# A two-layer expert network on one core: fetching one of each token's two answers during the last expert

## The chip, the cores and the metric

The kernel runs on one core of a Trainium2 chip. A core has five engines with queues of their own: TensorE (PE; its weight loads are listed as PEld), VectorE (DVE), ScalarE (ACT), GpSimd (POOL) and SyncE (SP). Each engine works its queue off in order. Transfers are started from the queues of SP, ACT and POOL and are carried out by 16 DMA engines that all queues share. The metric is the device time of one execution in microseconds, as the median over runs.

## The reference, cut to what matters

Eight sequences of 100 tokens (800 tokens of width 512) pass through two layers. Each layer has a cross-attention and then an expert network in which a router picks two of eight experts for each token. The first expert network is the one at issue:

```python
xf = layernorm(x) * gamma + beta
probs = softmax(xf @ Wg.T + bg)
tp, ti = top_k(probs, 2)
tp = tp / (sum(tp) + 1e-8)
w = sum(one_hot(ti, 8) * tp[..., None], axis=1)
h = gelu(einsum('td,efd->tef', xf, W1) + b1)
y = einsum('tef,edf->ted', h, W2) + b2
x = x + einsum('ted,te->td', y, w)
```

A token needs the answers of its two experts only, each times its own weight. After this comes the second layer's cross-attention, which begins with a layer norm of the new `x`.

## The kernel before

Everything is in float32. The 800 tokens lie in seven tiles of 128 rows (the last one has 32), and `x` stays in SBUF all the time.

**Routing (class Route).** As the tokens' tiles are ready, `group` finds for each token its best and its second expert, works out a row number in a table for each, and sends the normalised token to both rows with indirect DMAs from the POOL queue (L267). `where[0]` and `where[1]` hold these row numbers and `m[0]`, `m[1]` the weights: index 0 is the better expert of a token, index 1 the second best. The table `sent` and the table of results, `answers`, have 800 rows for each expert.

**Order of the experts.** `order` (L274) counts the tokens of each expert and numbers the experts by size: the one with most tokens gets slot 0 and is worked off first, that with the fewest gets slot 7. The weights are prefetched in this order through a pool of eight tiles, from SP's queue.

**Working the experts off (`work_off`, L379).** For each slot, `arrived` fetches the tokens' rows from `sent` and turns them into columns. `hidden0` makes the hidden activations on PE and ACT in four groups of matmuls. After the first group it calls `between`, which turns the previous expert's result back into rows and writes it to `answers` from the POOL queue (`returned`, L377). `products` makes the second matmul. When the loop is through, the last expert's result is written.

**The conditional rest (`rest`, L394).** If an expert has more tokens than its slot holds, a conditional block works the remainder off. With these inputs it is jumped over. On the way past it each engine makes up for the semaphore counts of the block that it skipped (events at L397), and POOL first waits for all transfers of its own queue.

**Between the expert layer and the attention.** `project_early` (L449) makes keys and values of five units of the second batch's context for the attention that follows: for each unit 2 x 4 matmuls into PSUM (L425), two ACT copies to `mT` (L429), six transposes (L437), three ACT copies to `mv` (L439 to L442) and three stores from ACT's queue. In the same stretch both answers of each token are fetched from `answers` (`fetch`, L333, an indirect DMA from POOL's queue), two fetches for each of the seven tiles, and DVE adds each of them, times its weight, to `x` (L723). Then each tile gets its moments (L127, L129), a square root on ACT (L137), its normalised copy `xn` (L146), four transposes on PE (L157) and four ACT evictions into `xT1` (L166). POOL adds the output bias to `x` (L729). A scheduler of the framework interleaves the instructions of this stretch on each engine; what it put first on an engine's queue blocks what it put behind.

The tiles for the fetched rows have two buffers, each with room for both answers of a token tile. The `xn` tiles have two buffers as well, and so have the small tiles of factors.

The second layer's attention begins with the query projection (L414), which needs `xT1` whole.

Of the kernel before, what the change touches and what calls it, by code (L numbers as in the profile page):

```python
# [13 lines left out]
P = 128  # L14
# [52 lines left out]
def two_layers(ctx: ExitStack, tc: tile.TileContext, a: dict, out: bass.AP):  # L67
# [137 lines left out]
    class Route:  # L205


        def __init__(self, layer, psum, tag):
            self.layer, self.psum, self.tag = layer, psum, tag
            self.logits = routes.tile([P, NTILE, NE], F32, tag="logits", name=f"logits{layer}")  # L210
            nc.vector.memset(self.logits, 0.0)
            self.m = [routes.tile([P, NTILE], F32, tag=f"m{k}", name=f"m{k}_{layer}") for k in range(2)]
            self.where = [
                routes.tile([P, NTILE], mybir.dt.int32, tag=f"where{k}", name=f"where{k}_{layer}") for k in range(2)
            ]
            self.sel = routes.tile([P, NTILE, NE], F32, tag="sel", name=f"sel{layer}")
# [6 lines left out]

        def largest(self, v, m, name):

            g = v.shape[1]
            nc.vector.tensor_reduce(m, v, AX.X, ALU.max)
            at = self.temp([P, NTILE, NE], f"at{name}")[:, :g, :]
            nc.vector.tensor_tensor(at, v, over_experts(m), ALU.is_equal)
            nc.vector.tensor_tensor(at, at, rank.unsqueeze(1).to_broadcast([P, g, NE]), ALU.mult)  # L230
            first = self.temp([P, NTILE], "first")[:, :g]
            nc.vector.tensor_reduce(first, at, AX.X, ALU.max)
            nc.vector.tensor_tensor(at, at, over_experts(first), ALU.is_equal)
            return at

        def group(self, i0, i1, xn):

            g, v = i1 - i0, self.logits[:, i0:i1, :]
            at1 = self.largest(v, self.m[0][:, i0:i1], 1)
            other = self.temp([P, NTILE, NE], "other")[:, :g, :]  # L240
            nc.vector.scalar_tensor_tensor(other, at1, -3e38, v, ALU.mult, ALU.add)
            at2 = self.largest(other, self.m[1][:, i0:i1], 2)
            full = g if i1 < NTILE else g - 1
# [30 lines left out]
        def order(self, load):  # L274
# [103 lines left out]

    def work_off(jobs, arrive, hidden, product, send_back, first=None, midway=None):  # L379

# [12 lines left out]

    def rest(more, work, first, second, bufs):  # L394

        v = nc.values_load(more[:1, :1], min_val=0, max_val=1)
        with tc.If(v > 0), tc.tile_pool(name="rest", bufs=bufs) as rp:  # L397

            def piece(w):
# [70 lines left out]
    with tc.tile_pool(name="a0", bufs=1) as ap, tc.tile_pool(name="a0w", bufs=3) as aw, tc.tile_pool(  # L470
# [184 lines left out]
        nc.vector.tensor_tensor(m1, m1, s, ALU.mult)  # L655
        nc.vector.tensor_tensor(m2, m2, s, ALU.mult)


    with f0, tc.tile_pool(name="f0w", bufs=2) as fw, tc.tile_pool(
# [28 lines left out]

        def work0(jobs, first=None, midway=None):
            work_off(  # L690
                jobs, lambda e, r0, n: arrived(0, e, r0, n, fw, ps, gamma0, beta0), hidden0,
                lambda e, n, h, w2: products(n, h, [w2(g) for g in range(NF // 4)], NF, fw, ps, b2s[:, e, :]),
                lambda e, r0, n, yT: returned(0, e, r0, n, yT, fp, ps), first, midway,
            )

        weights.limit = W_L1A + 4
# [5 lines left out]
            for e in range(NE)  # L702
        ], W_L0F, fetch_context)
        rest(
            more, work0, lambda piece, e, g: piece(of(0, "W1", e, g)), lambda piece, e, g: piece(of(0, "W2", e, g)), 4
        )

        bo = fw.tile([P, D], F32, name="bo", bufs=1)
# [8 lines left out]
        for i in range(NTILE):  # L717
            w = rows[i]
            both = fp.tile([P, 2, D], F32, tag="nil", name="back0", bufs=2)
            for k, m in enumerate((m1, m2)):  # L720
                y = both[:, k]
                fetch(y, where, i, k)
                nc.vector.scalar_tensor_tensor(  # L723
                    x[:w, i, :], y[:w], m[:w, i : i + 1], x[:w, i, :], ALU.mult, ALU.add
                )
            xn = fp.tile([P, D], F32, tag="mv", name="xn1", bufs=2)
# [344 lines left out]
```

## Time and profile before

| | |
|---|---|
| median of 3 runs | 1884.36 us (1884.31 to 1885.33) |
| profiled execution | 1883.63 us |
| its span (first to last instruction) | 1882.0 us |
| granted TensorE clock, mean | 0.959 |
| PE busy | 1725.5 us, 92% of the span |
| DVE busy | 594.9 us, 32% |
| ACT busy | 479.7 us, 25% |
| POOL busy | 147.8 us, 8% |

The profile is one execution. Busy time of PE is the time in which matmuls are in the array, and their ends are modelled. A line of the timeline shows the start, the duration, the engine, the source line, what is written from what, how many instructions were merged, and in brackets how long the engine had been idle before and what released it. A line of the table by windows shows the stretch, its length, then for PE, PEld, DVE, ACT and POOL the busy time and the count, then the granted clock as a share of full speed, the DMA share and GB/s. A line of the waits shows who waited for whom, the total in us, how many times, and the longest. A `q` after an engine's name stands for its sequencer.

### The profile page before, as it was taken

What the parts mean: (1) busy time and instruction counts of PE and PEld (TensorE: products, weight loads), DVE (VectorE), ACT (ScalarE), POOL (GpSimd) and SP (SyncE); (2) the same over time, 40 slices, a digit from 0 to 9 for tenths busy, and PEclk for the clock granted to TensorE, in tenths of its full rate; (3) what the DMA queues carried; (4) which work ended last, traced back from release to release, by engine and by line L of the source; (5) the groups of instructions that cost most, each with busy time, mean ns of one, the idle gap of its engine ahead of it and who ended that gap; (6) DMA issues with size and microseconds to landing.
All of it is one profiled execution on the core that took longest, in us unless ns stands there. A gap on an engine that the chain in (4) does not pass through costs nothing. (4 is left out here: it accounts for less than half of the span.)

```text
span 1882.0 us, 26422 instructions
## 1 busy us (share of the span) xinstructions
PE 1725.5 (92%) x10414; PEld 1306.4 (69%) x10414; DVE 594.9 (32%) x1462; ACT 479.7 (25%) x1400; POOL 147.8 (8%) x237
## 2 busy tenths in 40 slices
PE   5999689999999879999999999999999849999990
PEld 2455479999999645666666666666666528999990
DVE  4464510011111220454344424444444331111115
ACT  2364211111111132333333323333333210010110
POOL 4010310000000220000000000000000030000003
PEclk9999889999999989999999999999999969999995
DMA  9901374465555361131020300202201145555523
GB/s 367 414 28 56 124 284 169 182 222 189 203 201 219 108 235 45 40 96 56 5 37 5 59 3 5 37 6 37 27 6 15 6 159 221 192 185 200 207 79 114
DMA packets 74657, 227.87 MB, mean 121 GB/s; under 512 B 26273, under 2 KB 37161, under 8 KB 58129
## 3 DMA queue, kind: packets, MB, share of 16 engines
q1 hardware_dynamic: 53020, 177.98, 27.7%
q0 software_dynamic: 9888, 30.06, 5.1%
q10 hardware_dynamic: 11604, 17.95, 3.2%
q8 instruction: 86, 1.41, 0.3%
q14 instruction: 59, 0.48, 0.1%
HBM read 177.12 MB, written 48.83 MB: 120 GB/s over the span
## 5 line engine op out<-in xcount | busy, mean ns | idle before, releaser
L425 PE MATMUL ps_m<-cb,w 128*128 128x361 f32 x944 | 315.7, 486 | 0.0
L356 PE MATMUL ps_y<-h,w 128*128 128x256 f32 (+7 forms) x1536 | 280.5, 344 | 0.0
L356 PEld LDWEIGHTS ps_y<-h,w 128*128 128x128 f32 x1536 | 268.6, 190 | 7.9
L425 PEld LDWEIGHTS ps_m<-cb,w 128*128 128x128 f32 x944 | 180.5, 196 | 110.5 <-issue 18.0
L680 PE MATMUL ps_h<-xgT,w 128*128 128x256 f32 (+7 forms) x1024 | 189.5, 346 | 0.0
L680 PEld LDWEIGHTS ps_h<-xgT,w 128*128 128x128 f32 x1024 | 180.8, 192 | 5.8
L784 ACT ACTIVATE pr<-ps_sc,m 100x822 f32<-100x822 f32 x128 | 119.9, 942 | 175.7 <-issue 89.9
L808 DVE COPY prT<-ps_ptA 128x500 f32<-128x500 f32 x128 | 82.1, 678 | 187.1 <-PE ps_ptA L807 187.1
L782 DVE TENSOR_REDUCE m<-ps_sc 100x1 f32<-100x822 f32 x128 | 123.8, 1009 | 46.7 <-PE ps_sc L778 46.7
L684 ACT ACTIVATE h<-ps_h,s_b 128x256 f32<-128x256 f32 (+7 forms) x128 | 56.1, 438 | 303.8 <-PE ps_h L680 303.8
L429 ACT COPY mT<-ps_m 128x361 f32<-128x361 f32 x128 | 58.8, 460 | 251.5 <-PE ps_m L425 226.1
L414 PE MATMUL ps_col<-xT,w 128*128 128x400 f32 x320 | 115.1, 518 | 1.3 <-ACT xT L166 1.3
L950 PE MATMUL ps_g<-xgT,w 128*128 128x256 f32 (+7 forms) x512 | 104.3, 347 | 0.0
L950 PE MATMUL ps_u<-xgT,w 128*128 128x256 f32 (+7 forms) x512 | 102.8, 344 | 0.0
L414 PEld LDWEIGHTS ps_col<-xT,w 128*128 128x128 f32 x320 | 61.9, 197 | 47.3 <-issue 4.2
L950 PEld LDWEIGHTS ps_g<-xgT,w 128*128 128x128 f32 x512 | 91.4, 192 | 3.0
L950 PEld LDWEIGHTS ps_u<-xgT,w 128*128 128x128 f32 x512 | 90.7, 190 | 2.7
L778 PE MATMUL ps_sc<-mT,qT 64*100 64x311 f32 (+1 forms) x512 | 91.3, 468 | 0.0
L828 PEld LDWEIGHTS ps_av<-prT,mv 128*64 128x64 f32 (+1 forms) x1536 | 67.9, 137 | 31.3 <-issue 28.9
L955 ACT ACTIVATE sg<-ps_g 128x256 f32<-128x256 f32 (+7 forms) x64 | 22.3, 348 | 238.8 <-PE ps_g L950 238.8
L828 PE MATMUL ps_av<-prT,mv 128*64 128x100 f32 (+1 forms) x1536 | 80.6, 253 | 0.0
L807 PEld LDWEIGHTS ps_ptA<-ident,pr 100*128 100x128 f32 x640 | 65.2, 141 | 20.7 <-issue 10.6
(242 smaller groups left out, 1799.6 us busy)
## 6 DMA issues: line engine op xcount, KB each, us to landing
w<-in_W SPq DMA_DIRECT2D x64, 1024.0 KB
w<-in_w_gate SPq DMA_DIRECT2D x16, 1024.0 KB
w<-in_w_up SPq DMA_DIRECT2D x16, 1024.0 KB
w<-in_w_down SPq DMA_DIRECT2D x16, 1024.0 KB
sent<-nil SPq DMA_DIRECT2D x25, 512.0 KB
answers<-nil SPq DMA_DIRECT2D x25, 512.0 KB
cb<-in_ctxT ACTq DMA_DIRECT2D x16, 722.0 KB
xg<-sent POOLq DMA_DIRECT2D x18, 256.0 KB
```

What stands on the lines that cost most here:

```text
L356: nc.tensor.matmul(py[:, k, :n], ws[f // 4][:, f % 4, dc * P : (dc + 1) * P], h[:, f, :n], start=f == 0, stop=f == nf - 1,)
L414: nc.tensor.matmul(ps[:, :HALF], w[c // 4][:, dc, (c % 4) * P : (c % 4 + 1) * P], xT[:, dc, cols], start=dc == 0, stop=dc == DC - 1,)
L425: nc.tensor.matmul(pm[:, : S // 2], w_m[ic // 4][:, dc, (ic % 4) * P : (ic % 4 + 1) * P], cb[h][:, dc, : S // 2], start=dc == 0, stop=dc = ...
L429: nc.scalar.copy(mT[:, h * (S // 2) : (h + 1) * (S // 2)], pm[:, : S // 2])
L680: nc.tensor.matmul(ph[:, :n], w[:, dc, j * P : (j + 1) * P], xg[:, dc, :n], start=dc == 0, stop=dc == DC - 1,)
L778: nc.tensor.matmul(sc[:, bank, c0:c1], qT[r, ic, q0 : q0 + T], keys_, start=True, stop=True)
L782: nc.vector.tensor_reduce(m, sc[:, :, :NKH], AX.XY, ALU.max, negate=True)
L784: nc.scalar.activation(pr.rearrange("p (a n) -> p a n", a=2), sc[:, :, :NKH], AF.Exp, bias=m, accum_out=sums[:, j : j + 1],)
L807: nc.tensor.transpose(pt[:, c, :], pr[:, T + c * P : T + (c + 1) * P], ident[:T, :T])
L808: nc.vector.tensor_copy(prT[:, : NSC - 1, :], pt)
L828: nc.tensor.matmul(po[r, 0, :], vj, prT[j][:w, c, :], start=c == 0, stop=c == NSC)
L950: nc.tensor.matmul(p_[:, :n], w_[:, dc, j * P : (j + 1) * P], xg[:, dc, :n], start=dc == 0, stop=dc == DC - 1,)
```

## The change

Each token's two answers are put in the order in which they are made. A new method `by_slot`, called once the weights of the first expert layer are ready, looks up the slot of both experts of each token; where the first index has the later slot, it swaps the row numbers and the weights of the two, so that index 0 is the answer that is made first. For that, `Route` keeps the one-hot choices (`at`) and the row numbers in float (`places`) instead of temporary tiles.

The answers with index 0 can all come from slots 0 to 6. They are fetched by seven indirect DMAs that are issued during the last expert, after its first group of hidden matmuls and after the write of the seventh expert's result; they land in seven tiles of their own. Behind the conditional block DVE adds them to `x`. The later stretch then has one fetch and one addition for each tile instead of two. If the conditional block is run, the seven fetches are made again at its end.

```diff
@@ class Route
+            self.at, self.places = (
+                [routes.tile(shape, F32, tag=f"{t}{k}", name=f"{t}{k}_{layer}") for k in range(2)]
+                for t, shape in (("at", [P, NTILE, NE]), ("place", [P, NTILE]))
+            )
...
-                place = self.temp([P, NTILE], "place")[:, :g]
+                place = self.places[k][:, i0:i1]
...
-            slot = self.temp([P, NE], "slot")
+            slot = self.slot = self.temp([P, NE], "slot")
...
+        def by_slot(self, behind):
+
+            wide = self.temp([P, NTILE, NE], "pick")
+            nc.gpsimd.tensor_copy(wide[:1, 0, :1], behind[:1, :1])
+            slots = [self.temp([P, NTILE], f"slots{k}") for k in range(2)]
+            for at, t in zip(self.at, slots):
+                nc.vector.tensor_tensor(wide, at, self.slot.unsqueeze(1).to_broadcast([P, NTILE, NE]), ALU.mult)
+                nc.vector.tensor_reduce(t, wide, AX.X, ALU.add)
+            swap = slots[0]
+            nc.vector.tensor_tensor(swap, slots[0], slots[1], ALU.is_gt)
+            for pair in (self.places, self.m):
+                d = slots[1]
+                nc.vector.tensor_tensor(d, pair[1], pair[0], ALU.subtract)
+                nc.vector.tensor_tensor(d, d, swap, ALU.mult)
+
+                other = self.temp([P, NTILE], "first")
+                nc.vector.tensor_tensor(other, pair[1], d, ALU.subtract)
+                nc.vector.tensor_tensor(pair[0], pair[0], d, ALU.add)
+                nc.vector.tensor_copy(pair[1], other)
+            for k in range(2):
+                nc.vector.tensor_copy(self.where[k], self.places[k])
...
-            h = hidden(e, n, x, w1, lambda: done and send_back(*done))
+            last = k + 1 == len(jobs)
+            h = hidden(e, n, x, w1, lambda: (done and send_back(*done), last and ahead and ahead()))
...
+            again()
...
         nc.vector.tensor_tensor(m2, m2, s, ALU.mult)
+        route.by_slot(where[1])
...
+        firsts = turned_x.tile([P, NTILE - 1, D], F32, tag="xT", name="firsts")
+        firsts = [firsts[:, i] for i in range(NTILE - 1)]
+        SHORT_AT = rows.index(min(rows))
+        firsts.insert(SHORT_AT, fp.tile([P, D], F32, tag="o_b1", name="first_short"))
+
+        def fetch_firsts():
+            for i in range(NTILE):
+                fetch(firsts[i], where, i, 0)
...
-        ], W_L0F, fetch_context)
+        ], W_L0F, fetch_context, fetch_firsts)
...
+        for i, w in enumerate(rows):
+            nc.vector.scalar_tensor_tensor(
+                x[:w, i, :], firsts[i][:w], m1[:w, i : i + 1], x[:w, i, :], ALU.mult, ALU.add
+            )
...
-            both = fp.tile([P, 2, D], F32, tag="nil", name="back0", bufs=2)
-            for k, m in enumerate((m1, m2)):
-                y = both[:, k]
-                fetch(y, where, i, k)
-                nc.vector.scalar_tensor_tensor(
-                    x[:w, i, :], y[:w], m[:w, i : i + 1], x[:w, i, :], ALU.mult, ALU.add
-                )
+            y = fp.tile([P, D], F32, tag="nil", name="back0", bufs=2)
+            fetch(y, where, i, 1)
+            nc.vector.scalar_tensor_tensor(
+                x[:w, i, :], y[:w], m2[:w, i : i + 1], x[:w, i, :], ALU.mult, ALU.add
+            )
```

More of the change, by code (lines that the diff above doesn't have):

```diff
@@ L222, in temp, with largest @@
             return routes.tile(shape, type, tag=name, name=f"{name}_{self.layer}")
-        def largest(self, v, m, name):
+        def largest(self, v, m, at):
             g = v.shape[1]
             nc.vector.tensor_reduce(m, v, AX.X, ALU.max)
-            at = self.temp([P, NTILE, NE], f"at{name}")[:, :g, :]
             nc.vector.tensor_tensor(at, v, over_experts(m), ALU.is_equal)
@@ L238, in group @@
             g, v = i1 - i0, self.logits[:, i0:i1, :]
-            at1 = self.largest(v, self.m[0][:, i0:i1], 1)
+            at1 = self.largest(v, self.m[0][:, i0:i1], self.at[0][:, i0:i1, :])
             other = self.temp([P, NTILE, NE], "other")[:, :g, :]
             nc.vector.scalar_tensor_tensor(other, at1, -3e38, v, ALU.mult, ALU.add)
-            at2 = self.largest(other, self.m[1][:, i0:i1], 2)
+            at2 = self.largest(other, self.m[1][:, i0:i1], self.at[1][:, i0:i1, :])
             full = g if i1 < NTILE else g - 1
@@ L377, in returned, with work_off @@
             nc.gpsimd.dma_start(out=rows_of(answers, layer, e, r0 + s * P, w), in_=y[:w])
-    def work_off(jobs, arrive, hidden, product, send_back, first=None, midway=None):
+    def work_off(jobs, arrive, hidden, product, send_back, first=None, midway=None, ahead=None):
         (x, raw), done = arrive(*jobs[0][:3]), None
@@ L392, in work_off, with rest @@
         send_back(*done)
-    def rest(more, work, first, second, bufs):
+    def rest(more, work, first, second, bufs, again=lambda: None):
         v = nc.values_load(more[:1, :1], min_val=0, max_val=1)
@@ L687, in hidden0, with work0 @@
             return h
-        def work0(jobs, first=None, midway=None):
+        def work0(jobs, first=None, midway=None, ahead=None):
             work_off(
@@ L692, in work0 @@
                 lambda e, n, h, w2: products(n, h, [w2(g) for g in range(NF // 4)], NF, fw, ps, b2s[:, e, :]),
-                lambda e, r0, n, yT: returned(0, e, r0, n, yT, fp, ps), first, midway,
+                lambda e, r0, n, yT: returned(0, e, r0, n, yT, fp, ps), first, midway, ahead,
             )
+        firsts = turned_x.tile([P, NTILE - 1, D], F32, tag="xT", name="firsts")
[5 more added lines that the diff above has]
+                fetch(firsts[i], where, i, 0)
         weights.limit = W_L1A + 4
@@ L702, in two_layers @@
             for e in range(NE)
-        ], W_L0F, fetch_context)
+        ], W_L0F, fetch_context, fetch_firsts)
         rest(
-            more, work0, lambda piece, e, g: piece(of(0, "W1", e, g)), lambda piece, e, g: piece(of(0, "W2", e, g)), 4
+            more, work0, lambda piece, e, g: piece(of(0, "W1", e, g)), lambda piece, e, g: piece(of(0, "W2", e, g)), 4, fetch_firsts,
         )
+        for i, w in enumerate(rows):
+            nc.vector.scalar_tensor_tensor(
+                x[:w, i, :], firsts[i][:w], m1[:w, i : i + 1], x[:w, i, :], ALU.mult, ALU.add
+            )
         bo = fw.tile([P, D], F32, name="bo", bufs=1)
```

## The prediction, made before the changed kernel was run

> **What bounds the kernel now.** The page shows PE busy for 92% of the span, so I looked for the stretch in which PE waits because of the fetches. They start at 638.76 us and the attention's first projection at 684.38 us. The table by windows of this stretch comes first:
>
> ```profile
> 628.50:638.70 10.20, 8.09 (x31) 4.91 (x30) 0.67 (x2) 1.72 (x5) 1.08 (x2) 1.00 0.23 80
> 638.70:647.00 8.30, 3.69 (x14) 1.96 (x12) 3.61 (x6) 2.38 (x5) 5.48 (x6) 0.98 0.58 177
> 647.00:655.00 8.00, 6.07 (x19) 3.83 (x20) 4.44 (x12) 2.22 (x8) 4.26 (x5) 0.81 0.70 220
> 655.00:663.00 8.00, 6.02 (x25) 3.79 (x26) 5.43 (x14) 2.02 (x6) 5.90 (x6) 1.00 0.73 229
> 663.00:671.00 8.00, 7.21 (x24) 4.25 (x23) 4.27 (x8) 2.57 (x8) 2.69 (x6) 0.79 0.69 228
> 671.00:684.40 13.40, 5.09 (x29) 3.53 (x29) 5.44 (x12) 10.71 (x33) 6.52 (x5) 0.74 0.74 294
> ```
>
> No engine is full in any of the first five windows, so this is a chain of waits; in the sixth ACT is at 10.71 of 13.40 us. The waits of 620 to 690 us name the links:
>
> ```profile
> DVE x L723 <- DMA back<-answers,where: 20.5, 6, 14.2
> ACT rb L137 <- DVE mv_a L129: 14.2, 4, 5.0
> PE ps_mv L437 <- ACT mT L429: 9.5, 5, 4.7
> ```
>
> DVE waits for fetched rows, ACT's square root waits for DVE's moments, and PE waits for `mT`, whose copy stands behind that square root in ACT's queue. The timeline shows it three times:
>
> ```profile
> 638.76 1.05 POOL L333 DMA_INDIRECT back<-answers,where  x1 [5.80 <-ACT mv L442]
> ...
> 643.32 1.54 DVE L723 SCALAR_TENSOR_TENSOR x<-back,m,x 128x512 f32<-128x512 f32 x2 [14.15 <-DMA back<-answers,where]
> ...
> 646.37 0.29 ACT L137 ACTIVATE rb<-mv_a,eps 128x1 f32<-128x1 f32 x1 [5.00 <-DVE mv_a L129]
> ...
> 647.07 1.11 PE L437 MATMUL ps_mv<-ident,mT 128*128 128x128 f32 x4 [4.68 <-ACT mT L429]
> ...
> 654.21 0.29 ACT L137 ACTIVATE rb<-mv_a,eps 128x1 f32<-128x1 f32 x1 [4.14 <-DVE mv_a L129]
> ...
> 654.91 0.66 PE L437 MATMUL ps_mv<-ident,mT 128*128 128x128 f32 x4 [1.86 <-ACT mT L429]
> ...
> 661.94 0.29 ACT L137 ACTIVATE rb<-mv_a,eps 128x1 f32<-128x1 f32 x1 [4.05 <-DVE mv_a L129]
> ...
> 662.63 0.66 PE L437 MATMUL ps_mv<-ident,mT 128*128 128x128 f32 x4 [1.98 <-ACT mT L429]
> ```
>
> The first stall is the landing of the first fetch, the other two the third and fourth token tiles, whose fetches had to wait for a buffer. PE loses 4.68, 1.86 and 1.98 us. In the last unit, where no square root stands ahead, the same wait is 0.33 us (timeline at 669.79 us): that is what remains of each without a stall.
>
> **The change, part by part.**
>
> *by_slot.* It adds 17 DVE instructions and one POOL copy. Rows of the routing give 0.21 us for an operation on 128x56, 0.19 for a reduction of it, 0.16 for one on 128x7: 2 x 0.21 + 2 x 0.19 + 13 x 0.16 = 2.9 us. They come after the biases of the experts are sorted (DVE ends at 231.7 us). Where they end up:
>
> ```profile
> 236.78 1.18 POOL L344 DMA_DIRECT2D xg<-sent  x2 [5.39 <-issue]
> ...
> 240.96 2.64 DVE L164 TENSOR_SCALAR xgT<-ps_tp,p_gamma,p_beta 128x128 f32<-128x128 f32 x8 [9.25 <-PE ps_tp L157]
> ```
>
> DVE is idle for 9.25 us there. The two casts that rewrite `where` have to wait until the last sends have read it; the first expert's load at 236.78 us waits for the same sends, and DVE's next work needs that load. So I take 0. Without this cover it would be 2.9 us. The POOL copy can slip between two sends, which are on the path: 0 to 0.3 us by the 0.17 us of such a copy and its gap.
>
> *The seven early fetches.* They are queued on POOL behind the seventh expert's two writes, and since a fetch reads the whole table they wait until the second has landed. Behind them on POOL stands only the last expert's write, which in its turn waits for them. The timeline and the DMA share:
>
> ```profile
> 601.65 0.53 POOL L377 DMA_DIRECT2D answers<-y  x1 [7.34 <-DMA answers<-y]
> ...
> 628.88 0.54 POOL L377 DMA_DIRECT2D answers<-y  x1 [26.70 <-DVE y L376]
> ```
>
> ```profile
> 613.00:628.50 15.50, 15.50 (x104) 14.99 (x103) 2.03 (x6) 0.00 (x0) 0.00 (x0) 1.00 0.00 1
> ```
>
> The first write took about 7.3 us to land beside weight loads, so the second lands by 609. Seven fetches at the 1.27 us from start to start that the later ones show are issued by 618, and the last lands 4.6 us after its start (638.76 to 643.32), about 621.5. The write wants to go at 628.88 us, 7 us later, and DMA is empty from 613 on. Cost 0; POOL's other queued work (context, token loads) comes earlier. If the fetches took longer than the margin, each further us would be on the path.
>
> *The skipped block.* It grows by seven fetches that are never run. POOL needs 632.8 to 638.76 us for its branch, its catch-up and its waits already, and the catch-up is made once for each counter, not once for each transfer: 0.
>
> *Adding the early answers.* Seven DVE operations (0.75 us median of L723, 5.3 us together). Their operands could also have been written in the block, so they wait for POOL's catch-up, which released ACT at 637.80 us: DVE is done at 643.05, the first late answer lands at 643.32. Hidden, with 0.3 us to spare. At L723's mean of 0.82 us it would be 643.6, and 0.25 us late.
>
> A rule against this: the Trainium skill (Advanced Engine Details and Errata, VectorE Performance Modes, Mode Summary) says that VectorE's second SBUF port is shared with GpSimd and that their instructions can block each other. The additions read two SBUF tiles just when POOL prepares the first two late fetches. The trace shows how much: the fetch at 646.39 us took 1.47 instead of 0.95 us beside two such additions, the one at 645.13 us beside another took 0.95. So at most 0.5 us for the first fetch; I take 0, and keep 0.5 as a bound. Were the port held for all seven additions, as the rule's "block" could be read, the first fetch would be 4.3 us late and the gain below nearly gone; no row shows such a hold.
>
> *The first stall.* The first late fetch cannot start before 638.76 us, as the last expert's write still precedes it. After its landing one addition is saved, 0.77 us. The first square root comes at 645.6 instead of 646.37. I take 0.8; the bounds are -0.75 (both small delays above) and 4.35 (4.68 - 0.33, should the scheduler queue this square root behind the next `mT` copy).
>
> *The second and third stall.* The third tile's fetch needs a buffer, which is free when the first tile's addition is through: about 644.1 us instead of 645.1, and it is one fetch instead of two (the second one started at 646.39 and was added at 652.16). It lands about 648.9 and its moments are ready at 650.6 instead of 654.2, when PE has hardly finished the next matmuls. Likewise the fourth. Both stalls go: (1.86 - 0.33) + (1.98 - 0.33) = 3.2 us. Late next is PE's own chain of matmuls and transposes. Bounds: 0, if the scheduler moves the square roots up by as much, and 3.2.
>
> *The clock.* After the third stall the granted clock is 0.79 and 14 matmul records of L425 take 6.11 us, against 4.42 us in the window at clock 1.00. With PE less idle I expect full clock there: 1.7 us. Between 647 and 655 us the clock is 0.81 after the longest stall; that stall remains, and so does this. Bounds 0 and 2.8 (the first one costs 4.24 - 10 x 0.316 = 1.1).
>
> The Trainium skill's TensorE: Matmul & The Clock Gate (Part 1) holds that the clock drops after about 3.4 us of idling. By it the 2 us stalls would not matter and the term would be 0, the sum 4.0. The trace shows a drop after a 1.98 us stall and none after one of 1.86 us, so I go by the row but keep 0 in the range.
>
> *The tail*, 671 to 684.4 us: 28 evictions on ACT with square roots between them that wait for the two buffers of `xn`, not for fetches. The weights that wait for the last fetch (L56) are needed at 729 us and later. 0.
>
> Sum: 0.8 + 3.2 + 1.7 = 5.7 us. By the profiled execution (1883.63 us, its span 1882.0 and 1.6 around it) that gives 1877.9; the median of the runs lies 0.73 us higher: 1884.36 - 5.7 = 1878.7 us.
>
> **The rivals.**
>
> 1. *The scheduler keeps the waits.* With one fetch for each tile it may believe the moments ready sooner and queue the square roots ahead of earlier `mT` copies; ACT waits as long as before. For it: the order of before already put three of them too early. Against: the real data also come 1 to 6 us earlier. Only the first term remains: 1883.6, at best 1881.
>
> 2. *The first stall goes too*, if its square root ends up behind the copy: 4.35 + 3.2 + 2.8 = 10.4 us, 1874.0. For it: seven additions now stand ahead of the first tile on DVE also in the scheduler's eyes. Against: POOL's fetch is no sooner.
>
> 3. *Slower: the early fetches hold up the last write.* Because both go by the whole table, the write waits for all seven. If they went one after another at 4.6 us each, they would end at 609 + 32 = 641 us, 12.3 us after 628.88; less the 5.7 gained, 1891 us. It decides from the point where the last one lands 5.7 us after 628.88, at 634.6. For it: writes to the table wait for each other 13 times, 81.2 us in total. Against: the fetches of before ran four at a time, 1.27 us apart, into tiles of their own.
>
> That the change doesn't do what it says (fetches issued early, but executed late) could only be if the second write of the seventh expert landed after 628; it has 27 us.
>
> **How the numbers follow.** My forecast, a gain of 3.8 to 8 us, gets 0.52, rival 2 gets 0.13, rival 1 gets 0.22 and rival 3, with anything else that costs, 0.13. A change under 0.2% (3.8 us) can't be told from none. Faster: 0.52 + 0.13, of which 0.02 falls short, 0.63. Same: 0.02 + 0.22 = 0.24. Slower: 0.13. The range leaves out the best part of rival 2 and rival 3: 1872.5 to 1885.0.
>
> **What would show it.** Right: seven fetches (L333) between 609 and 622 us with the last write still at about 629; seven additions from 637.8; ACT's waits for L129 falling from 14.2 us to about 5, PE's for `mT` from 9.5 to about 5.5; the first L414 6 us earlier. Wrong: the last write later than 630, the waits for L129 still above 10 us, or a first L414 at 684.

## The result, and the profile after

| | before | after |
|---|---|---|
| median of 20 runs each, side by side | 1883.68 us | 1882.53 us |
| ratio | | 0.9991, interval 0.9985 to 0.9997 |
| profiled execution, its span | 1883.63 us, 1882.0 us | 1882.01 us, 1880.5 us |
| granted TensorE clock, mean | 0.959 | 0.959 |

The change brings 1.2 us where 5.7 were forecast. The time lies in the stated range of 1872.5 to 1885.0 us, but a gain of 0.1% is under the 0.2% that the prediction took as the least that can be told from none, and a repeat (e7) has 1 in its interval. In what follows "the stretch" is the time from the first write of the last expert's answers to the first matmul of the query projection: 628.88 to 684.38 us before (55.50 us), 626.39 to 679.50 us after (53.11 us). Lines are those of the new kernel: the fetch is L358 (was L333), the units' matmuls L452 (L425), the copy to `mT` L456 (L429), the transposes L464 (L437), the early additions L746, the late ones L763 (L723), the write of the answers L402 (L377), the query projection L441 (L414).

First the part that went as planned, from the timeline of the changed kernel around the early fetches:

```profile
598.83 0.54 POOL L402 DMA_DIRECT2D answers<-y  x1 [7.03 <-DMA answers<-y]
...
602.83 1.04 POOL L358 DMA_INDIRECT firsts<-answers,where  x1 [3.46 <-ACT h L712]
...
610.46 0.89 POOL L358 DMA_INDIRECT first_short<-answers,where  x1 [0.30 <-issue]
...
626.39 0.58 POOL L402 DMA_DIRECT2D answers<-y  x1 [15.04 <-DVE y L401]
```

All seven fetches are issued between 602.83 and 611.4 us, in the middle of the last expert. POOL then stands idle for 15.04 us, and what ends this idle time is DVE's `y`, not a fetch: the last expert's write is not held up.

Next the waits of 617 to 688 us, to be laid beside those of before (14.2, 9.5 and 20.5 us):

```profile
ACT rb L137 <- DVE mv_a L129: 10.9, 4, 5.1
...
DVE x L746 <- DMA firsts<-answers,where: 8.4, 1, 8.4
PE ps_mv L464 <- ACT mT L456: 8.3, 4, 6.0
...
DVE x L763 <- DMA back<-answers,where: 6.3, 4, 2.8
```

DVE's waits for fetched rows fell from 20.5 to 14.7 us. Of these, the 8.4 us put down to `firsts` is the skipped block (the seven fetches had been issued by 611.4 us), which before was part of the single wait of 14.2 us; the other waits for rows come to about 6.3 us both times. ACT's and PE's waits fell by 3.3 and 1.2 us only, and PE's longest one is now 6.0 instead of 4.7 us. The table by windows shows where (window, length; busy time of PE, PEld, DVE, ACT and POOL; clock, DMA share, GB/s):

```profile
626.00:636.20 10.20, 8.09 (x31) 4.90 (x30) 1.85 (x4) 1.74 (x5) 1.16 (x3) 1.00 0.23 80
636.20:644.50 8.30, 8.00 (x32) 4.79 (x30) 6.02 (x10) 3.58 (x7) 3.69 (x4) 1.00 0.64 204
644.50:650.00 5.50, 4.46 (x18) 2.97 (x19) 3.30 (x7) 2.21 (x7) 2.22 (x3) 1.00 0.77 258
650.00:658.00 8.00, 2.01 (x10) 1.25 (x9) 6.05 (x15) 0.94 (x3) 3.96 (x3) 0.78 0.16 48
658.00:665.80 7.80, 7.01 (x23) 4.11 (x21) 1.35 (x6) 2.48 (x8) 0.80 (x5) 0.79 0.87 306
665.80:679.50 13.70, 5.18 (x29) 3.62 (x29) 5.43 (x12) 10.83 (x33) 6.51 (x5) 0.71 0.59 242
```

The second window, where the first stall used to be, is now full of PE work: 8.00 of 8.30 us, against 3.69 of 8.30 before. Most of what was won there is lost in the fourth, where PE works 2.01 of 8.00 us. The timeline tells why:

```profile
635.03 4.07 DVE L746 SCALAR_TENSOR_TENSOR x<-firsts,m,x 128x512 f32<-128x512 f32 x6 [8.35 <-DMA firsts<-answers,where]
...
641.60 0.75 DVE L763 SCALAR_TENSOR_TENSOR x<-back,m,x 128x512 f32<-128x512 f32 x1 [1.85 <-DMA back<-answers,where]
...
644.85 0.29 ACT L137 ACTIVATE rb<-mv_a,eps 128x1 f32<-128x1 f32 x1 [2.10 <-DVE mv_a L129]
...
645.54 0.66 PE L464 MATMUL ps_mv<-ident,mT 128*128 128x128 f32 x4 [1.34 <-ACT mT L456]
...
648.31 0.69 DVE L127 BATCH_NORM_STATS2 st_a<-x 128x6 f32<-128x512 f32 x1
...
651.84 0.75 DVE L763 SCALAR_TENSOR_TENSOR x<-back,m,x 128x512 f32<-128x512 f32 x1 [2.84 <-DMA back<-answers,where]
652.51 0.16 DVE L140 RECIPROCAL rb<-rb 128x1 f32<-128x1 f32 x1
...
653.44 0.16 DVE L129 BATCH_NORM_AGGREGATE mv_a<-st_a 128x2 f32<-128x6 f32 x1
...
653.63 0.29 ACT L137 ACTIVATE rb<-mv_a,eps 128x1 f32<-128x1 f32 x1 [5.11 <-DVE mv_a L129]
653.76 1.62 POOL L769 TENSOR_TENSOR x<-x,bo 128x512 f32<-128x512 f32 x1
654.15 1.25 DVE L142 SCALAR_TENSOR_TENSOR tb<-mv_a,rb 128x1 f32<-128x1 f32 x1
...
656.58 0.30 ACT L137 ACTIVATE rb<-mv_a,eps 128x1 f32<-128x1 f32 x1 [2.65 <-DVE mv_a L129]
656.78 0.44 ACT L456 COPY mT<-ps_m 128x361 f32<-128x361 f32 x1
...
657.27 1.12 PE L464 MATMUL ps_mv<-ident,mT 128*128 128x128 f32 x4 [5.99 <-ACT mT L456]
...
658.18 5.95 PE L452 MATMUL ps_m<-cb,w 128*128 128x361 f32 x14
```

Read it backwards from 657.27. PE waits 5.99 us for `mT`. Its copy stands behind two square roots on ACT, those of the third and fourth tile. The third tile's square root waits 5.11 us for its moments, although the statistics of both tiles (L127) were finished by 649.0 us. Between 649.0 and 651.84 us DVE does nothing: the next instruction in its queue is the addition of the fifth tile, whose row is still on its way. Only behind that stands the first tile's reciprocal (L140), whose square root had been ready since 645.1, and behind this the third tile's aggregate (L129): it needs the small tile that the first tile's factors occupy, as there are two of them. So the fifth tile's row, whose own square root comes at 672 us, holds up the third tile. The fourth tile comes behind it in the same queue, and there about 1.1 us more are lost: the factors of the second tile (L142 at 654.15) take 1.25 us where the first tile's took 0.16 us at 652.70, and end at 655.40, as POOL's addition of the output bias does (655.38).

### The profile page after: what moved, and what is told of

The parts are those of the page before. It is cut to its first block, busy times and chain, and to the rows that moved or that the text cites. A ratio compares the mean times of both kernels' runs of the same rounds, so it can differ in the third digit from the quotient of the medians.

```text
span 1880.5 us, 26444 instructions
## 1 busy us (share of the span) xinstructions
PE 1725.2 (92%) x10414; PEld 1305.2 (69%) x10414; DVE 597.4 (32%) x1479; ACT 480.4 (26%) x1400; POOL 148.8 (8%) x238
## 5 line engine op out<-in xcount | busy, mean ns | idle before, releaser
L452 PE MATMUL ps_m<-cb,w 128*128 128x361 f32 x944 | 315.5, 486 | 0.0
L452 PEld LDWEIGHTS ps_m<-cb,w 128*128 128x128 f32 x944 | 180.3, 196 | 110.6 <-issue 17.9
L456 ACT COPY mT<-ps_m 128x361 f32<-128x361 f32 x128 | 58.9, 461 | 253.6 <-PE ps_m L452 228.1
L441 PE MATMUL ps_col<-xT,w 128*128 128x400 f32 x320 | 114.8, 517 | 1.3 <-ACT xT L166 1.3
L441 PEld LDWEIGHTS ps_col<-xT,w 128*128 128x128 f32 x320 | 61.7, 196 | 47.3 <-issue 4.0
L847 PEld LDWEIGHTS ps_ptA<-ident,pr 100*128 100x128 f32 x640 | 65.2, 141 | 20.7 <-issue 10.6
```

Source lines behind the costliest of these rows:

```text
L441: nc.tensor.matmul(ps[:, :HALF], w[c // 4][:, dc, (c % 4) * P : (c % 4 + 1) * P], xT[:, dc, cols], start=dc == 0, stop=dc == DC - 1,)
L452: nc.tensor.matmul(pm[:, : S // 2], w_m[ic // 4][:, dc, (ic % 4) * P : (ic % 4 + 1) * P], cb[h][:, dc, : S // 2], start=dc == 0, stop=dc = ...
L456: nc.scalar.copy(mT[:, h * (S // 2) : (h + 1) * (S // 2)], pm[:, : S // 2])
L847: nc.tensor.transpose(pt[:, c, :], pr[:, T + c * P : T + (c + 1) * P], ident[:T, :T])
```

## The experiments

**Theory.** The early fetches work and are free; their gain is eaten by the order in DVE's queue, where a late addition stands ahead of factors that were ready long before. **Rivals.** (B) The pace of the late fetches is at fault: two buffers, so the fifth row starts late. (C) The early fetches are worth nothing in any order, since something else sets the end of the stretch. (D) The reordering by slots costs what the fetches bring. Every experiment but e8 gives a ratio to the kernel before, from runs on the same chip, and each has one profile. "PE's waits" are those for `mT` in L464 (L437).

### e1: the order by slots alone

Both fetches are late again, as before, in the new order of index 0 and 1.

```diff
-        ], W_L0F, fetch_context, fetch_firsts)
+        ], W_L0F, fetch_context)
...
-        for i, w in enumerate(rows):
-            nc.vector.scalar_tensor_tensor(
-                x[:w, i, :], firsts[i][:w], m1[:w, i : i + 1], x[:w, i, :], ALU.mult, ALU.add
-            )
...
+            both = fp.tile([P, 2, D], F32, tag="nil", name="back0", bufs=2)
+            for k, m in enumerate((m1, m2)):
+                y = both[:, k]
+                fetch(y, where, i, k)
...
```

> The answers are put in slot order as in the change, but none is fetched early: both fetches of a token tile are made in the late stretch, as before. The stretch is the time from the last expert's first write to the answers to the first matmul of the query projection: 55.5 us in the profile of before, 53.1 in that of the change. Both theories expect that the slot order by itself costs nothing: stretch 55.5 +- 0.5 with three waits of PE for mT of about 4.7, 1.9 and 2.0 us, total time within 0.1% of before. If the 17 small DVE operations were on the path after all, the time would be 2 to 3 us above before, and the first expert's evictions would start that much later after its load.

Measured: ratio 0.9990 (0.9978 to 1.0001), stretch 52.58 us, PE's waits 0.64, 2.94, 2.54, 1.05 and 0.33 us. The order by slots costs nothing that shows; rival D falls. The stretch, expected at 55.5 +- 0.5 us, is 3 us shorter than that of the first profile of before, in a kernel that does the same work there, and PE's waits differ from the expected ones too, which was the first sign that single profiles of this stretch scatter by some 3 us (e8).

### e2: four late rows in flight

```diff
-            y = fp.tile([P, D], F32, tag="nil", name="back0", bufs=2)
+            if i % 2 == 0:
+                both = fp.tile([P, 2, D], F32, tag="nil", name="back0", bufs=2)
+            y = both[:, i % 2]
```

> The change, but the late answers of two token tiles share one buffer, so that four fetches can be in flight instead of two. Theory A (the gain was given back in DVE's queue: the fifth tile's addition stands ahead of the first tile's factors and waits for its rows, so the third tile's root comes late and holds up the mT copy behind it): in this kernel the additions of tiles five to seven still stand ahead of the first factors, so the rows come a little sooner but the seventh is waited for as well; one PE wait for mT of 3 to 6 us stays, stretch 51 to 54 us. Theory B (the fetches' own latency with two buffers is what counts): the fetches are through 4 to 5 us sooner, that wait shrinks below 2 us, stretch 48 to 50 us.

Measured: ratio 0.9997 (0.9987 to 1.0008), stretch 52.19 us, PE's waits 0.64, 3.98 and 0.33 us. The late rows do come sooner: the fifth is added 21.2 us after the last expert's first write (648.27 less 627.11) instead of 25.5 (651.84 less 626.39). But the timeline of this kernel shows the same picture, two tiles further:

```profile
651.57 0.74 DVE L765 SCALAR_TENSOR_TENSOR x<-back,m,x 32x512 f32<-32x512 f32 x1 [0.80 <-DMA back<-answers,where]
...
652.24 0.14 DVE L140 RECIPROCAL rb<-rb 128x1 f32<-128x1 f32 x1
...
653.35 0.29 ACT L137 ACTIVATE rb<-mv_a,eps 128x1 f32<-128x1 f32 x1 [3.71 <-DVE mv_a L129]
...
656.39 1.12 PE L464 MATMUL ps_mv<-ident,mT 128*128 128x128 f32 x4 [3.98 <-ACT mT L456]
```

Every addition now stands ahead of the first reciprocal, the seventh tile's included (presumably because the scheduler believes all rows to be early). A faster fetch does not help, so rival B falls as the main cause.

### e3 and e4: one square root for all tiles, behind the units

Here DVE collects the moments of all seven tiles in one small tile, and ACT takes a single square root behind the last unit's copies, so that no square root and no wait for one stands between the units. e3 does this to the changed kernel, e4 to the kernel before.

```diff
+        mvs = fp.tile([P, NTILE, 2], F32, name="mvs")
+        rs, ts = (fp.tile([P, NTILE], F32, name=n) for n in ("rs", "ts"))
...
+            st = small.tile([P, 6], F32, tag="st", name="st_a1")
+            nc.vector.bn_stats(st, x[:, i, :])
+            nc.vector.bn_aggr(mvs[:, i, :], st)
+        weights.limit = len(pieces)
+        weights.load(W_L1A + 8, y[:1, :1])
+        nc.scalar.copy(rs[:1, :1], made[-1][1][:1, 0, :1])
+        nc.scalar.activation(rs, mvs[:, :, 1], AF.Sqrt, bias=eps2, scale=1.0 + EPS)
+        nc.vector.reciprocal(rs, rs)
+        nc.vector.scalar_tensor_tensor(ts, mvs[:, :, 0], -1.0, rs, ALU.mult, ALU.mult)
+        for i in range(NTILE):
             xn = fp.tile([P, D], F32, tag="mv", name="xn1", bufs=2)
-            scaled(xn, x[:, i, :], *factors(moments(x[:, i, :], "a1"), "b", twice=True))
+            scaled(xn, x[:, i, :], rs[:, i : i + 1], ts[:, i : i + 1])
```

`made` holds the `mT` and `mv` tiles of the units, so `made[-1][1]` is the last unit's `mv`. The two `weights` lines stood at the end of the stretch and are moved up; the loads still wait for the last fetched row.

> The change, but the moments of all seven tiles go into one tile and a single square root for all of them is made on ACT behind the last unit's copies. No root stands ahead of an mT copy. Theory A (roots that wait in ACT's queue are what PE loses by): PE's waits for mT fall from 8.3 to about 2 us, the granted clock between the units stays near 1.00, the units end about 6 us sooner, the tail loses its 3.5 us wait for roots as well; stretch 43 to 47 us, total 6 to 10 us below before. Theory C (PE, ACT and the clock set the pace of the units whatever the roots do): PE's waits turn into waits for something else, stretch 51 to 54 us, total as the change.

> The kernel before, with the same single root behind the units: both answers are fetched late. It gives what the early fetches are worth when ACT waits for nothing. Theory A: the units run freely, but x is whole only about 28 us after the first late fetch (666 us in the profile of before), so the root and the tail start there; the stretch is 50 to 53 us, 5 to 8 us longer than with the early fetches. Theory C: the same stretch as the one-root form of the change, within 1 us.

Measured: e3 0.9962 (0.9948 to 0.9976), stretch 46.31 us, PE's waits 0.64 and 0.33 us. e4 0.9999 (0.9988 to 1.0011), stretch 53.08 us, PE's waits 1.74 and 0.33 us. From the second unit on PE loses nothing but the usual 0.33 us in either. The difference comes behind the units, where PE's first token transposes wait for the normalised tile and ACT's square root (with the load of its table ahead of it) waits for the last tile's moments (timelines, first e3, then e4):

```profile
660.38 1.28 ACT L780 ACT_TABLE_LOAD   x1 [1.60 <-DVE mvs L776]
...
663.13 1.94 PE L157 MATMUL ps_tp<-ident,xn 128*128 128x128 f32 x8 [5.88 <-DVE xn L146]
```

```profile
666.78 1.28 ACT L740 ACT_TABLE_LOAD   x1 [3.73 <-DVE mvs L736]
...
669.54 1.94 PE L157 MATMUL ps_tp<-ident,xn 128*128 128x128 f32 x8 [8.02 <-DVE xn L146]
```

Counted from the last expert's first write, the root's table load starts after 32.8 us in e3 and after 39.6 us in e4, which is the difference of the two stretches. (In e4's profile the units end 4.6 us later too, with longer waits and slower matmuls behind the skipped block; as ACT waits for the moments even so, that doesn't set the end.) With two late fetches a tile, e4 moves the waits from the units to their end and gains nothing. With one, e3 is 6.8 us shorter in the stretch and 0.4% in time. Rival C falls: the early fetches are worth about 7 us (0.0038 x 1885.49 = 7.2) where no queue order eats them.

### e5, e11, e12: the order in DVE's queue

One element written by DVE behind the factors of tile i (`mark`) is copied by POOL into the buffer of tile i + 4 before its fetch. So the scheduler can no longer put the additions of the fifth to seventh tile ahead of the first tiles' factors. The square roots keep their places in ACT's queue. e12 repeats e5; e11 makes the same edit in the kernel before.

```diff
+        mark = fp.tile([P, NTILE], F32, name="mark")
...
+            if i >= 4:
+                nc.gpsimd.tensor_copy(y[:1, :1], mark[:1, i - 4 : i - 3])
             fetch(y, where, i, 1)
...
-            scaled(xn, x[:, i, :], *factors(moments(x[:, i, :], "a1"), "b", twice=True))
+            r, t = factors(moments(x[:, i, :], "a1"), "b", twice=True)
+            nc.vector.tensor_copy(mark[:1, i : i + 1], t[:1, :1])
+            scaled(xn, x[:, i, :], r, t)
```

> The change, but the fetch of the fifth and later token tiles waits for the factors of the tile four before it (a one-element copy on POOL from a mark that DVE writes), so that DVE's queue has the first and second tile's factors ahead of the fifth tile's addition. Theory A (the fifth tile's addition, queued ahead, made the third root late): the third root comes at most 1.5 us after ACT is ready for it instead of 5.1, PE's longest wait for mT falls from 6.0 to below 2 us, stretch 48 to 50 us, total 3 to 5 us below the change. Theory C (the pace of the units and the clock): PE's waits change places, stretch 52 to 54, total as the change.

> The kernel before, with the order of e5_factors_first alone: the fetches of the fifth to seventh tile wait for a one-element mark of DVE behind the factors of the tile four earlier. If the gain of e5_factors_first is that of the early fetches, set free by the order, this gains nothing by itself: the first root is still late by the first tile's two fetches, stretch from the first write of the last expert's answers to the query projection 52 to 55.5 us, time within 0.15% of the kernel before. If the order alone carries it, the stretch is 47 to 48.5 us and the kernel 3 to 5 us faster, and the early fetches are worth nothing of their own.

> The kernel of e5_factors_first once more, on the chip of e11_before_factors_first, so that the difference of the two is what the early fetches are worth under one DVE order. Expected by the theory (early fetches plus order): stretch 46.5 to 47.5 us, TensorE's waits for mT under 2 us, 3 to 6 us below the kernel before. By the rival (a chance of one profile): stretch above 50 us again.

Measured: e5 0.9974 (0.9963 to 0.9985), stretch 46.84 us, PE's waits 0.64, 0.44 and 0.33 us. e12 0.9972 (0.9959 to 0.9985), stretch 46.43 us, PE's waits 0.64, 1.52, 0.53 and 0.33 us, 3.0 in sum where under 2 were expected. e5's stretch is shorter than the 48 to 50 us that were expected. e11 0.9998 (0.9989 to 1.0007), stretch 53.69 us, PE's waits 0.64, 3.01, 2.81, 1.64 and 0.33 us. The timeline of e5 at the place of the long wait:

```profile
649.84 0.15 DVE L140 RECIPROCAL rb<-rb 128x1 f32<-128x1 f32 x1
...
650.82 0.15 DVE L129 BATCH_NORM_AGGREGATE mv_a<-st_a 128x2 f32<-128x6 f32 x1
...
651.00 0.29 ACT L137 ACTIVATE rb<-mv_a,eps 128x1 f32<-128x1 f32 x1 [1.67 <-DVE mv_a L129]
...
652.53 0.66 PE L464 MATMUL ps_mv<-ident,mT 128*128 128x128 f32 x4 [0.44 <-ACT mT L456]
```

The factors of the first tile no longer wait for the fifth tile's row, the third tile's square root waits 1.67 instead of 5.11 us (1.5 were expected at most), and PE 0.44 instead of 5.99 us. The fifth row even comes later than in the change: its fetch starts 24.6 us after the last expert's first write (651.14 less 626.56) instead of 20.7 (647.10 less 626.39). The early fetches and the order of DVE's queue make a square of four kernels, as ratios to the kernel before:

| | order as the scheduler makes it | factors ahead of later additions |
|---|---|---|
| both answers late | 1 | 0.9998 (e11) |
| one answer early | 0.9991, 0.9998 (e7) | 0.9974 (e5), 0.9972 (e12) |

Neither does much alone; together they give 4.9 to 5.3 us (0.0026 x 1885.84 and 0.0028 x 1885.91). This shows the theory: same fetches, same buffers, same additions, another order in DVE's queue. The one-element copies that make the order (seven on DVE, three on POOL) bring nothing by themselves, as e11 shows. The second tile's factors, too, now come ahead of POOL's addition and take 0.16 us instead of 1.25.

### e6 and e9: four rows in flight and one square root

e6 joins the edits of e2 and e3. e9 changes one more line: the loads of the second layer's weights (`in_Wkv`), which have been tied to the last fetched row, are tied to the last unit's `mv` instead (its expectation calls this the last tile's moments).

```diff
-        weights.load(W_L1A + 8, y[:1, :1])
+        weights.load(W_L1A + 8, made[-1][1][:1, 0, :1])
```

> The one-root form of the change with four late fetches in flight instead of two. There the root still waited 1.6 us for the last tile's moments, and two buffers held the fetches up. Theory A: the moments are whole 4 to 5 us sooner, the root follows the last unit's copies at once, stretch 44.5 to 45.5 us instead of 46.3, total 1 to 2 us below the one-root form (some 8 to 9 us below before). If the units' own chain already ended last, nothing changes: 46.3.

> The kernel with one root and four late answers in flight, with the second layer's first loads of w (in_Wkv) tied to the last tile's moments in place of its first answer, so that they start after the last late fetch has been worked off. If their collision with the stores of kept keys and values was what held the mT copy for 6.5 us, that wait is gone, TensorE waits under 1.5 us for mT, the stretch from the first write of the last expert's answers to the query projection is 44.5 to 45.5 us and the whole kernel 8 to 9.5 us below the kernel before. If it was something else, the stretch stays near 48 us and the wait stands elsewhere. If the held loads are then late themselves, the second layer's key and value matmuls wait for w, which the stretch alone does not show but the time does.

Measured: e6 0.9970 (0.9960 to 0.9980), stretch 48.19 us where 44.5 to 45.5 were expected: no better than e3. The timeline of e6 shows what the faster fetch set off:

```profile
653.72 6.52 ACTq L474 DMA_DIRECT2D kept_values<-mv  x2
...
655.07 1.92 SPq L58 DMA_DIRECT2D w<-in_Wkv  x4
...
660.33 0.82 ACT L456 COPY mT<-ps_m 128x361 f32<-128x361 f32 x2 [6.48 <-DMA w<-in_Wkv]
...
660.85 1.54 PE L464 MATMUL ps_mv<-ident,mT 128*128 128x128 f32 x6 [3.47 <-ACT mT L456]
```

The last row lands sooner, so four weight loads start 26.1 us after the last expert's first write (655.07 less 629.00), inside the last unit; in e3 it was 30.8 us. The line of 6.52 us merges the issues of two stores, which themselves are short (timeline in narrower windows):

```profile
653.72 0.33 ACTq L474 DMA_DIRECT2D kept_values<-mv  x1
...
659.98 0.25 ACTq L474 DMA_DIRECT2D kept_values<-mv  x1
```

Behind the other units the two are through in 0.67 to 0.93 us. Here 5.9 us pass between them, and ACT stands idle for 6.48 us before the copy to `mT`. In e9 the same loads start 30.3 us after that write (657.22 less 626.91), behind the last unit's transposes:

```profile
655.89 0.66 PE L464 MATMUL ps_mv<-ident,mT 128*128 128x128 f32 x4 [0.33 <-ACT mT L456]
...
657.22 2.37 SPq L58 DMA_DIRECT2D w<-in_Wkv  x4
```

The wait is gone (0.33 us) and the stretch is 44.68 us, as expected, so the early start of the loads is what held ACT up in e6 (one profile each). How they held the store isn't shown: in the changed kernel, e7, e10 and e11 two stores that were issued 0.1 to 0.3 us after the same loads began took 0.67 to 0.69 us. The time is not as expected: 0.9966 (0.9955 to 0.9977), 6.4 us below before where 8 to 9.5 were expected.

### e7, e8 and e10: repeats

The changed kernel, the kernel before and e3 again, unchanged.

> The change itself, a second profile and times beside the two above. The same order of instructions, so the same waits: a wait of PE for mT of 4 to 6.5 us ahead of the fourth unit's transposes, a stretch of 51.5 to 54.5 us, a time 0 to 3 us below before. If the long wait is a chance of this one profile, it will be missing here.

> The kernel before, a second profile of its stretch. The slots-only kernel has the same order of instructions as before, but its stretch was 52.6 us against 55.5. If a stretch varies that much from one execution to the next, this one falls between 52 and 56 us and the waits for mT between 7 and 10 us in total, and a difference of 2 us between two profiles shows nothing. If the stretch is steady, it is 55.5 +- 0.5.

> The kernel of e3_one_root once more, beside e9_root_four_held on one chip. If 46.31 us was no chance of one profile: stretch 45.5 to 47 us, TensorE's waits for mT 1 to 1.5 us, 6 to 8.5 us below the kernel before. If e9_root_four_held is below it by more than 1 us, the fetches' pace was still worth something behind the one root; if the two are equal, the end of the units and not the last fetch sets the root.

Measured: e7 0.9998 (0.9989 to 1.0007), stretch 53.44 us, PE's waits 0.64, 1.44, 5.88 and 0.33 us. The long wait is no accident of one profile. e8, one execution, has a stretch of 52.97 us and PE's waits of 0.64, 4.44, 0.88, 2.02 and 0.33 us, and behind the third stall it has full clock:

```profile
661.93 0.66 PE L437 MATMUL ps_mv<-ident,mT 128*128 128x128 f32 x4 [2.02 <-ACT mT L429]
...
662.42 4.42 PE L425 MATMUL ps_m<-cb,w 128*128 128x361 f32 x14
```

So the 55.50 us that the prediction started from were on the long side. In the two repeats PE's waits are 8.3 us before and 8.3 us after. e10 has 0.9960 (0.9945 to 0.9975) and 45.00 us, a little under the expected 45.5 to 47; its median, 1877.53 us, is that of e9, 1877.17 us. By e10's expectation that would mean that the end of the units sets the root's start, and not the last fetch. The trace doesn't say so: the root still waits for the last tile's moments, 1.60 us in e3 and here

```profile
661.15 1.28 ACT L780 ACT_TABLE_LOAD   x1 [0.68 <-DVE mvs L776]
```

Only in e9 does it follow the units at once (658.09 us, without a wait). So the pace of the late rows is still worth 0.7 to 1.6 us of the stretch in these profiles, too little for the times to show. The kernels with one root (e3, e9, e10) have the lowest ratios, but their intervals overlap those of e5 and e12.

## Why the prediction was right on the costs and wrong on the gain

The time fell into the range because the range also took in rival 1; the way in which the forecast gain of 3.8 to 8 us was to come about did not come true. Of the prediction's own signs of being wrong, one came: ACT's waits for L129 stayed above 10 us (10.9).

- **Order by slots, 0:** right. The second cast waits 2.27 us for the sends as foreseen, DVE is done at 234.5 us, and its next work starts at 238.43 and waits for PE. e1 agrees.
- **Early fetches, 0, and rival 3:** right, and earlier than predicted. I took 7.3 us for the landing of the seventh expert's second write, because its first had held up the second so long; the first fetch started 4.0 us after that write (602.83 less 598.83).
- **Skipped block, 0:** right. POOL's first late fetch starts 9.79 us after the last expert's first write; before it was 9.88.
- **Early additions, 0:** right, with more to spare. The first six took 4.07 us, 0.68 each instead of 0.75, and the last was done at 639.7; the first late row came at 641.60, a margin of 1.9 instead of 0.3 us. The two late fetches beside these additions took 1.14 and 0.99 us, against 1.05 and 0.97 us in the kernel before, with DVE idle. The port rule that I weighed (the Trainium skill, Advanced Engine Details and Errata, VectorE Performance Modes, Mode Summary) speaks of blocking between GpSimd and VectorE instructions in a mode with two ports. What the runs show of it here is 0.1 us at most for these two fetches, not the hold of 4.3 us that the strict reading would have given. Where POOL does arithmetic, a hold shows in the other direction: the 1.25 us of L142 beside the bias addition, above, which the prediction did not ask about.
- **First stall, 0.8:** the wait fell by 3.3 us (4.68 to 1.34), but not for my reason. The first square root came no sooner: 18.46 us after the last expert's first write, against 17.49 before. The scheduler had put the second tile's addition ahead of the first tile's moments, and moved that square root back by one unit, behind the `mT` copy of which my upper bound of 4.35 us and rival 2 spoke. In the second unit, where the 4.68 us had stood, PE no longer waits at all; the 1.34 us stand in the third unit.
- **Second and third stall, 3.2:** this is the step that failed. I read correctly that the third tile's row would land sooner (its addition ran at 646.08 us, 19.7 us after the last expert's first write; I had 20.0) and concluded that its moments would follow. They did not, because in an in-order queue it is not enough that an operand is there. The two stalls, 3.84 us, became one of 5.99 us, in the fourth unit. I had named the scheduler in rival 1, but looked for it in ACT's queue; the square roots moved back there. It was DVE's queue, of which I asked only what it had to compute, not in which order. With that order mended (e5, e12) the change gives 4.9 to 5.3 us. That this is near my 5.7 is partly luck: the sum holds 1.7 us of clock that the next point takes back, and leaves 3.9 us of the first stall in place, where e5 and e12 have at most 1.5 us.
- **Clock, 1.7:** wrong. The slow matmuls behind the 1.98 us stall were a matter of that profile; behind 2.02 us in e8 there are none. The page against which I weighed the row (the Trainium skill, TensorE: Matmul & The Clock Gate, Part 1) has the clock drop after about 3.4 us of idling. All other waits for `mT` from the second unit on agree with it. After 2.81, 2.94 and 3.01 us (e11, e1, e11) the next ten or fourteen matmuls run at full speed, 0.32 us each; after 3.47 us and more (e6, e2, e8, before, e7 and after) they or the transposes are slower, for instance 5.95 us for fourteen instead of 4.42. By these rows the page's 0 would have been the better term, and 4.0 the sum. (The matmuls behind the skipped block don't follow so simple a rule; see the last section.) The new wait of 5.99 us has a price in clock of its own, 1.5 us on these fourteen.
- **Tail, 0:** right, 13.7 against 13.5 us.
- **Rivals.** Rival 1 had the right outcome, a gain of 0.8 to 3.4 us (measured 1.2), and the right culprit, the scheduler, but the wrong queue: the square roots did not move ahead of earlier copies. Rival 2 came true in its first term alone. Rival 3's condition, a last row landing after 634.6 us, was never near.

What stays open: e9's stretch is 1.6 us shorter than e3's and 0.3 us shorter than e10's, and its time is no better. Single profiles can't follow that: from the query projection to the end of the span it is 1202.7 us in e9, 1199.6 in e3 and 1203.0 in e10, and e3 and e10 are the same kernel. And the first late row, once early additions run, is added 5.05 to 5.82 us after its fetch starts in all of these kernels but e5 (4.30), against 4.56 to 4.95 us without. The units' stores, which now run beside it in most of them, may be a cause, but this was not tested, and e2 speaks against it as the whole cause: there the row was added 5.15 us after its fetch, at 642.29 us, before the second unit's values were stored (642.44).

## What to carry to other kernels

When an operand comes sooner, ask of every engine on the way which instruction stands ahead of the one that uses it, and what that instruction waits for; an earlier transfer can lead a scheduler to queue a late consumer ahead of an early one. A data dependence of one element is enough to mend such an order, and to test whether the order is the cause. And take a term from a single profile (a clock drop, a stall of 2 us) only after asking how much the same stretch scatters between two executions.

## What the runs showed of the hardware that was not expected

- The same instructions can find another clock. The fourteen matmuls behind the skipped block took 4.42 us in nine of the fourteen profiles and 5.7 to 6.2 us in the other five (e1, e2, e4, e5, e11). Two short waits of PE stand ahead of them, with one transpose between: 0.64 us (1.74 in e4), and then 1.25 to 1.93 us in the nine and 1.73 to 2.67 us in the five. The longer wait mostly goes with the slow matmuls, but not always: 1.73 us was followed by slow ones in e2 and by fast ones in e6, and 1.93 us by fast ones in e3 and e7.
- Of two stores in ACT's queue, the second was issued 6.3 us after the first when four weight loads from SP's queue were started in between (e6). With these loads held back by 4.2 us, counted from the last expert's first write, both were through in 0.69 us and the wait was gone (e9).
- A small operation of VectorE can last as long as GpSimd's arithmetic beside it: L142 on 128x1 takes 0.16 us at 652.70, and 1.25 us at 654.15 and 675.56, each time ending with POOL's bias addition (L769, begun at 653.76 and 675.53).
- Two writes of one expert to the same table, from one queue: the first (591.26 us) held the second for 7.0 us, the second held the fetch behind it for at most 4.0 us.
